# An earlier and denser routing of the third token block inside an attention loop

## The chip, the cores and the metric

The kernel runs on one core of a Trainium2 chip. The metric is the device time of one execution in microseconds (us). Before the change three runs took 1201.39, 1204.87 and 1204.54 us, a median of 1204.54 us.

The core's engines each have an in-order instruction queue of their own: PE (matrix products and transposes), DVE (vector operations), ACT (activations), POOL (general operations, and the DMAs that scatter or gather rows by an index), and SP, which issues the plain DMAs.

## The reference: what is computed

The reference adds four layers to `x`, each on normalised rows: an attention (2 sequences of 1024 tokens, 16 heads of 8), a mixture of 160 experts of which each token uses 8, a recurrent memory layer, and a second mixture of 8 experts. All is float32. The change touches the first two:

```python
scores = einsum('bhqd,bhkd->bhqk', qh, kh) * scale * decay      # decay by distance
x = x + einsum('bhqk,bhkd->bhqd', softmax(scores), vh) @ Wo
xn = layernorm(x)
probs = sigmoid(xn @ router_w.T + expert_bias)
top_w, top_idx = top_k(probs, 8)
h1 = silu(einsum('th,eih->eti', xn, w_gate))
x = x + routed(h1, top_w * 2.5, w_down, top_idx) + shared(xn)
```

## The kernel before

The 2048 tokens are 16 tiles of 128 rows, in four blocks of four tiles. A block's tokens can be routed as soon as their attention is done. Routing a block gives each of its tokens eight row numbers in a large buffer `xs` in HBM, ordered by expert: pages of 128 rows. Sending a token means copying its normalised row to those eight places. POOL does this: one indirect DMA sends 128 rows (one tile, one of its eight choices), so a block takes 32 such DMAs. In what follows, "a row" is one of these DMAs with the small memset (line 770) ahead of it. When all four blocks are sent, the experts work page by page.

**The attention** (`attention_bounded`) works in 16 units: a unit is 512 queries of one sequence and four heads. The loop over `s` runs through software-pipelined steps, nine to a unit; `u, k = divmod(s, 9)` is the unit whose exponentials are made, and `v` is the unit, 11 steps ahead, whose score maxima are made. The order of instructions is the one in which the code is written. One step does the following:

- `exps` and `largest`, in two halves: PE makes score tiles (L400); ACT exponentiates those of unit `u` (L383), DVE takes the maxima of unit `v` (L333). The maxima end with step 132.
- `product`, three steps later: PE multiplies by the values (L412). The partial results of even `k` are added by DVE (L422); those of odd `k` are copied by ACT from PSUM to the tile `part` (L425), of which there is one buffer, and added to `od` by POOL (L426). At `k` = 8 POOL adds the two sums (L428).
- at `k` = 5, `sums` of the unit before: PE collects the softmax denominators, DVE inverts them, and POOL spreads them over the partitions' columns (L438, `rb`). At `k` = 8, `divided` uses them on PE and DVE.
- once in each unit, `shift`: POOL adds the maxima to the queries (L305, L306).

The loop's end (after step 147) is `sums` and `divided` for the last unit, the rows that are still to be sent of those planned for the loop, and the last projection (L456, L459).

**Routing in the loop.** `route0(i, ...)` is a generator with 16 steps for block `i`. In order: 1, a reciprocal root on DVE; 2 and 3, two normalised tiles each on ACT (L659); 4, four transposes; 5 and 6, the router's products; 7, a clamp on POOL (L679); 8, two ACT passes for the sigmoid (L681, L682); 9 and 10, the top eight of two tiles each on DVE (L685, L686); 11 and 12, counts and positions by matrix products with four ACT passes in all (L706, L707); 13 and 14, page arithmetic on DVE; 15, an addition on POOL (L728); 16, the row numbers `idx` on DVE (L732). The blocks 0, 1 and 2 begin behind steps 47, 83 and 119, and the list `when` says at which distance from there a step of the generator is taken: one a step, 16 in a row. PSUM tiles of the generator come from the pool `ps_b`, four buffers that the exponentials' scores and the products use too.

**Sending in the loop.** `scattered(i, first, end)` is a generator with one row in each step (L770, L771). From step 64 on one row is sent behind each step: the formula gives the number of blocks that may send, and the first block with rows left sends one. Block 0 has the steps 64 to 95, block 1 the steps 100 to 131, block 2 the steps 136 to 143. Of block 2 the loop is given `SENT` rows: 12.

**Behind the attention** block 3 is routed by the same generator, with no attention beside it. Around it stand, in the order of the code: its first step, the loads of the expert weights (SP, L1441 and L1442, behind a DVE memset at L1439), the remaining rows of block 2 on POOL (`behind`, 32 - `SENT` of them), the shared expert of blocks 0 and 1 between the route's steps (L989 to L1001), then 32 rows of block 3 on POOL, which wait for L732. The load of the first page (SP, L1035) waits for the rows of all blocks.

Of the kernel before, what the change touches and what calls it, by code (L numbers as in the profile page):

```python
# [20 lines left out]
NB = T // 512  # L21
# [9 lines left out]

NE, INTER0 = 160, 64
ROUTED_SCALE = 2.5
SENT = 12
GAP = 6
SOME = 88
MORE = 128
# [139 lines left out]
def attention_bounded(tc, small, xnT, wq_sb, wkc, wvc, wo_sb, ident, x_sb, ln_stats,  # L177
# [11 lines left out]
    with tc.tile_pool(name="bw", bufs=1) as bw, tc.tile_pool(name="bk", bufs=1) as bk, \  # L189
# [58 lines left out]
        def second():  # L248

            own = x_sb[:, KT:NT, :]  # L250
            x1 = be.tile([P, KT, P], F32, tag="e", name="x1")
            nm, r, sq = [bq.tile([P, KT], F32, tag=f"s{n}", name=f"s{n}", bufs=1)
                         for n in range(3)]
            for i in range(KT):
                nc.scalar.activation(x1[:, i, :], own[:, i, :], AF.Identity,
                                     accum_out=nm[:, i : i + 1])
                if i == 3:
                    yield
            nc.vector.tensor_scalar(nm, nm, -1.0 / P, None, ALU.mult)
            yield  # L260
            for i in range(KT):
                nc.scalar.activation(x1[:, i, :], own[:, i, :], AF.Square,
                                     bias=nm[:, i : i + 1], accum_out=sq[:, i : i + 1])
            yield
            nc.scalar.activation(r, sq, AF.Sqrt, scale=1.0 / P, bias=eps_t)
            nc.vector.reciprocal(r, r)
            nc.vector.tensor_mul(nm, nm, r)
            yield
            for blk in range(2):
                pt = ps_b.tile([P, 512], F32, tag="b", name="pt")  # L270
                for j in range(4):
                    i = 4 * blk + j
                    nc.scalar.activation(x1[:, i, :], own[:, i, :], AF.Identity,
                                         scale=r[:, i : i + 1], bias=nm[:, i : i + 1])
                    nc.tensor.transpose(pt[:, j * P : (j + 1) * P], x1[:, i, :], ident)
                nc.scalar.copy(xnT[:, S + blk * 512 : S + (blk + 1) * 512], pt)
                yield
# [70 lines left out]
        def other(u):  # L348

            b, qb, g = units[u]  # L350
            ps = [pair("so") for _ in range(2)]
            for r in range(4):
                cols = slice(r * P, r * P + P)
                keys_of = slice((4 * qb + r) * P, (4 * qb + r) * P + P)
                for half in range(2):
                    for j in range(2):
                        rows = rows_of(half, j)
                        nc.tensor.matmul(ps[half][:, j, cols], ku[b, g][rows, keys_of],
                                         qu[u][rows, cols], start=True, stop=True)
            eo[u] = be.tile([P, 4, 512], F32, tag="eo", name="eo", bufs=1)  # L360
            for half in range(2):
                nc.scalar.activation(eo[u][:, 2 * half : 2 * half + 2, :], ps[half], AF.Exp)

        def exps(u, k, half):

            b, qb, g = units[u]
            kt = tile_of(u, k)
            if half == 1:
                es[u, k] = be.tile([P, 4, 512], F32, tag="e", name="e")
            e = es[u, k]  # L370
            ps = [ps_b.tile([P, 512], F32, tag="b", name="sb") for _ in range(2)]
            a = min(max(kt - 4 * qb, 0), 4) * P
            todo = []
            for k_, q_, lo, hi in ((ku, qu, 0, a), (kl, ql, a, 512)):
                for j in range(2):
                    if lo < hi:
                        rows = rows_of(half, j)
                        todo.append((ps[j][:, lo:hi], k_[b, g][rows, kt * P : (kt + 1) * P],
                                     q_[u][rows, lo:hi]))

            def after():
                for j in range(2):
                    nc.scalar.activation(e[:, 2 * half + j, :], ps[j], AF.Exp)  # L383

            return todo, after

        def whole(u, k):

            cols = slice((k - FIRST) * P, (k - FIRST + 1) * P)
            nc.vector.copy_predicated(es[u, k][:, :, cols],  # L390
                                      upp.bitcast(I32).unsqueeze(1).to_broadcast([P, 4, P]),
                                      eo[u][:, :, cols])

        def both(*work):

            work = [w for w in work if w]
            for n in range(0, max((len(w[0]) for w in work), default=0), 2):
                for w in work:
                    for out, lhs, rhs in w[0][n : n + 2]:
                        nc.tensor.matmul(out, lhs, rhs, start=True, stop=True)  # L400
            for w in work:
                w[1]()
# [27 lines left out]
        def sums(u):  # L430
            ps = ps_b.tile([P, 512], F32, tag="b", name="ps_r")[:, 0:16]
            for i in range(4):
                nc.tensor.matmul(ps[:, 4 * i : 4 * i + 4], os[u][:, i * P : (i + 1) * P],
                                 ident[:, HD::32], start=True, stop=True)
            ri = bo.tile([P, 16], F32, tag="ri", name="ri")
            nc.vector.reciprocal(ri, ps)
            ris[u] = bo.tile([P, 16, 32], F32, tag="rb", name="rb", bufs=1)
            nc.gpsimd.tensor_copy(ris[u], ri.unsqueeze(2).to_broadcast([P, 16, 32]))  # L438
# [13 lines left out]
        def projected(u, po):  # L452
# [8 lines left out]
            for i in range(4):  # L461
# [4 lines left out]
        LEAD, N, U = 11, 9, len(units)  # L466

        when = [1, 2, 3, 4, 5, 6, 7, 8, 9, 10, 11, 12, 13, 14, 15, 16]  # L470
        routes = [route0(i, lambda name: ps_b.tile([P, 512], F32, tag="b", name=name))
                  for i in range(NB - 1)]
        sent = [scattered(i, 0, 32 if i < NB - 2 else SENT) for i in range(NB - 1)]
        others = second()
        keys(0, 0)
        queries(0)
        end = N * U
        for s in range(-LEAD, end + 4):
            v, i = divmod(s + LEAD, N)
            u, k = divmod(s, N)  # L480
            second = 0 <= s < end and k > 0
            first = v < U and k > 0
            i8 = i - (i > 2)
            if i == 0 and 1 <= v <= U:
                nc.vector.tensor_reduce(pad[:, :, :, HD], mp.pop(v - 1), AX.X, ALU.max, negate=True)
            both(exps(u, k, 1) if second else None, largest(v, i8, 0) if first else None)
            if 0 <= s - 2 < end and 0 <= (s - 2) % N - FIRST < 4:
                whole(*divmod(s - 2, N))
            if 0 <= s - 3 < end and (s - 3) % N:
                product(*divmod(s - 3, N))  # L490
            if k == 0 and 0 <= s < end:
                other(u)
            if i == 2 and v + 1 < U:
                queries(v + 1)
            both(exps(u, k, 0) if second else None, largest(v, i8, 1) if first else None)
            if i == 0 and 1 <= v <= U:
                shift(v - 1)
            if k == 5 and 1 <= u < U:
                sums(u - 1)
            if k == 8 and 1 <= u < U:  # L500
                divided(u - 1)
            if v == 0 and i != 3:
                next(others, None)
            if v == 0 and i in (3, 8):
                values(i // 8)
            if i == 4 and 0 <= v < NG - 1:
                keys(0, v + 1)
            if k == 4 and 5 <= u < 5 + NG:
                keys(1, u - 5)
            if i == 4 and u - 2 >= 0 and units[u - 2][2] == NG - 1:  # L510
                projected(u - 2, pair("po")[:, 0, :])
            for blk in range(NB - 1):
                o = s - (N * (4 * blk + 5) + 2)
                for _ in range(when.count(o)):
                    next(routes[blk])
            blk = (s - (N * 5 + 2 + when[-1] + 1)) // (4 * N)
            if 0 <= blk < NB and s < end:
                for g in sent[: blk + 1]:
                    if next(g, sent) is not sent:
                        break  # L520
        sums(U - 1)
        divided(U - 1)
        for g in sent:
# [6 lines left out]
def model(ctx, tc, x, wq, wk, wv, wo, wdown, wupk, wupv, rw, ebias, wg, wd, wgs, wds,  # L530
# [249 lines left out]
    with tc.tile_pool(name="aw", bufs=1) as aw:  # L780
# [150 lines left out]
        with cond.Else():  # L931
# [11 lines left out]
            with tc.tile_pool(name="ps_r", bufs=4, space=PSUM) as ps_r:  # L943
                for i in range(NB - 1):
                    for _ in route0(i, lambda name: ps_r.tile([P, 512], F32, tag="r", name=name)):
                        pass
                    for _ in scattered(i, 0, 32 if i < NB - 2 else SENT):
                        pass
# [6 lines left out]
    with tc.tile_pool(name="fw", bufs=1) as fw, tc.tile_pool(name="fs", bufs=3) as fs, \  # L955
# [477 lines left out]
        with tc.manual_schedule():  # L1433
            last = route0(NB - 1, lambda name: ps_g.tile([P, 512], F32, tag="g", name=name))
            behind = scattered(NB - 2, SENT, 32)
            beside = [shared(i) for i in range(NB)]
# [186 lines left out]
```

## Time and profile before

One execution was profiled: its span, from the first to the last instruction, is 1197.7 us, and its own time was 1199.52 us, 5.0 us below the median of the runs.

| engine | busy us | share of the span |
|---|---|---|
| PE (products) | 990.6 | 83% |
| DVE | 766.8 | 64% |
| ACT | 627.8 | 52% |
| POOL | 538.1 | 45% |

The moments of this execution that matter here, in us from the span's start:

| moment | us |
|---|---|
| first exponential of step 131 (L383) | 566.2 |
| row numbers of block 2 (L732) | 586.5 |
| first exponential of step 143 | 607.5 |
| last spread of reciprocals (L438) begins | 617.53 |
| `x` complete (L459) begins | 624.01 |
| first weight load issued (L1441) | 636.99 |
| row numbers of block 3 (L732) | 661.35 |
| last row of block 3 begins (L771) | 702.87 |
| first page load issued (L1035) | 705.36 |

A profile line of the group view gives the line of the code, the engine, the operation, the names of what it writes and reads, the shapes and the count; then the busy time and the mean of one in ns; then the idle time of its engine just before it and who ended it. A line of the view in order of time gives start, duration, engine, line and operation, with the idle time ahead in brackets. "Clock" is the share of full speed that the chip granted to PE.

### The profile page before, as it was taken

What the parts mean: (1) busy time and instruction counts of PE and PEld (TensorE: products, weight loads), DVE (VectorE), ACT (ScalarE), POOL (GpSimd) and SP (SyncE); (2) the same over time, 40 slices, a digit from 0 to 9 for tenths busy, and PEclk for the clock granted to TensorE, in tenths of its full rate; (3) what the DMA queues carried; (4) which work ended last, traced back from release to release, by engine and by line L of the source; (5) the groups of instructions that cost most, each with busy time, mean ns of one, the idle gap of its engine ahead of it and who ended that gap; (6) DMA issues with size and microseconds to landing.
All of it is one profiled execution on the core that took longest, in us unless ns stands there. A gap on an engine that the chain in (4) does not pass through costs nothing. (4 is left out here: it accounts for less than half of the span.)

```text
span 1197.7 us, 20714 instructions
## 1 busy us (share of the span) xinstructions
PE 990.6 (83%) x7721; PEld 631.2 (53%) x7721; DVE 766.8 (64%) x1756; ACT 627.8 (52%) x1302; POOL 538.1 (45%) x657
## 2 busy tenths in 40 slices
PE   5899999998999999999972437888743479999998
PEld 2544444444444444554341226666632368888887
DVE  5788888677877798877534216555533457777643
ACT  3577777565766656666732014443322345666652
POOL 4345333344775735645556742232326565553000
PEclk9999999998999999999995558888775579999999
DMA  7999500000000000000007536776534212222110
GB/s 220 284 285 246 118 1 1 1 1 1 15 21 17 19 5 19 19 19 16 13 23 265 169 112 218 240 227 224 179 136 149 74 44 77 78 78 67 41 49 36
DMA packets 120334, 113.99 MB, mean 95 GB/s; under 512 B 50016, under 2 KB 102368, under 8 KB 118560
## 3 DMA queue, kind: packets, MB, share of 16 engines
q1 hardware_dynamic: 110496, 92.61, 25.3%
q0 software_dynamic: 9728, 19.94, 5.8%
q8 instruction: 66, 1.08, 0.4%
q14 instruction: 44, 0.36, 0.1%
HBM read 65.26 MB, written 57.74 MB: 103 GB/s over the span
## 5 line engine op out<-in xcount | busy, mean ns | idle before, releaser
L333 DVE TENSOR_REDUCE mp<-sa 128x2 f32<-128x1024 f32 x248 | 299.0, 1220 | 99.3 <-PE sa L400 94.1
L383 ACT ACTIVATE e<-sb 128x512 f32<-128x512 f32 x512 | 272.3, 601 | 116.5 <-PE sa L400 102.5
L400 PE MATMUL sa<-kl,ql 32*128 32x512 f32 (+3 forms) x752 | 172.3, 538 | 7.1 <-DVE mp L333 4.2
L400 PE MATMUL sb<-ql,kl 32*128 32x512 f32 (+3 forms) x768 | 171.1, 509 | 5.6 <-DVE o L422 3.7
L1407 POOL DMA_INDIRECT gt<-ys,idxu x128 | 122.6, 958 | 113.2 <-SPq L1473 25.4
L400 PE MATMUL sb<-qu,ku 32*128 32x512 f32 (+3 forms) x640 | 141.1, 507 | 6.0 <-DVE o L422 4.1
L412 PE MATMUL o_ps<-e,vv 128*32 128x512 f32 x1024 | 139.1, 616 | 3.8 <-DVE e L390 3.0
L400 PE MATMUL sa<-ku,qu 32*128 32x512 f32 (+3 forms) x612 | 124.5, 485 | 0.5 <-DVE mp L333 0.3
L400 PEld LDWEIGHTS sb<-ql,kl 32*128 32x128 f32 x768 | 74.3, 187 | 67.7 <-ACT e L383 32.7
L771 POOL DMA_INDIRECT xs<-xn,idxu x96 | 98.0, 1021 | 20.9 <-issue 17.7
L400 PEld LDWEIGHTS sb<-qu,ku 32*128 32x128 f32 x640 | 59.3, 185 | 88.9 <-ACT e L383 64.9
L1045 POOL DMA_INDIRECT wx<-wt,widx x48 | 46.0, 959 | 112.0 <-PE pt_x L1070 99.2
L426 POOL TENSOR_TENSOR od<-od,part 128x512 f32<-128x512 f32 x48 | 64.9, 1352 | 34.4 <-ACT part L425 34.0
L1373 ACT ACTIVATE hh_g<-gg_ps 128x512 f32<-128x512 f32 x64 | 37.9, 591 | 78.3 <-PE gg_ps L1360 62.9
L1364 PE MATMUL og_ps<-hw_g,w_sb 128*128 128x256 f32 x256 | 67.8, 388 | 3.9 <-DVE hw_g L1380 3.4
L1360 PE MATMUL u_ps<-xc,w_sb 128*128 128x256 f32 x256 | 69.2, 393 | 1.5 <-DVE xc L1355 1.3
L400 PEld LDWEIGHTS sa<-kl,ql 32*128 32x128 f32 x752 | 58.7, 186 | 21.1 <-DVE mp L333 9.3
L1360 PE MATMUL gg_ps<-x2T,w_sb 128*128 128x256 f32 x256 | 69.3, 395 | 0.0
L1380 DVE TENSOR_TENSOR hw_g<-hh_g,u_ps 128x512 f32<-128x512 f32 x64 | 43.7, 683 | 39.4 <-PE u_ps L1360 25.2
L1421 DVE SCALAR_TENSOR_TENSOR x_sb<-gt,w,x_sb 128x128 f32<-128x128 f32 x128 | 44.7, 350 | 29.8 <-DMA gt<-ys,idxu 25.4
L1070 PE MATMUL pt_x<-ident,xp 128*128 128x128 f32 x248 | 41.9, 322 | 26.5 <-DMA xp<-xs 24.4
L1127 DVE COPY y<-y_ps 128x512 f32<-128x512 f32 x31 | 21.4, 690 | 64.5 <-remote 29.9
(349 smaller groups left out, 1910.5 us busy)
## 6 DMA issues: line engine op xcount, KB each, us to landing
xs<-zeros SPq DMA_DIRECT2D x16, 1152.0 KB
xp<-xs SPq DMA_DIRECT2D x31, 512.0 KB
ys<-y SPq DMA_DIRECT2D x31, 512.0 KB
cb<-cD SPq DMA_DIRECT2D x8, 1024.0 KB
wt<-in_wg SPq DMA_DIRECT2D x4, 1280.0 KB
wt<-in_wd SPq DMA_DIRECT2D x8, 640.0 KB
wg_sb<-in_wg SPq DMA_DIRECT2D x4, 1280.0 KB
ys<-zeros SPq DMA_DIRECT2D x5, 512.0 KB
```

The lines of the kernel that those rows point to most:

```text
L333: nc.vector.tensor_reduce(mp[u][:, qt, 2 * half : 2 * half + 2, kb], pa, AX.X, ALU.max)
L383: nc.scalar.activation(e[:, 2 * half + j, :], ps[j], AF.Exp)
L400: nc.tensor.matmul(out, lhs, rhs, start=True, stop=True)
L412: nc.tensor.matmul(o_ps[32 * j : 32 * j + 32, :], vvs[b][:, kt, h : h + 2, :].rearrange("p a b -> p (a b)"), e[:, j, :], start=True, stop= ...
L426: nc.gpsimd.tensor_add(od[u], od[u], part)
L771: s = nc.gpsimd.indirect_dma_start(xs, bass.IndirectOffsetOnAxis(ap=idx[:, 4 * i + j, k : k + 1], axis=0), xn_[i][:, j, :], None).ins
L1045: dma = nc.gpsimd.indirect_dma_start(wx[:, q, :], None, wt, bass.IndirectOffsetOnAxis(ap=widx[:, c : c + 1], axis=0))
L1360: nc.tensor.matmul(ps[:, h, :], w13_sb[:, at : at + P], rhs, start=True, stop=True)
L1364: nc.tensor.matmul(o_ps, w2_sb[:, 2 * e + h, :], hw[e][:, h, :], start=(e == h == 0), stop=(e == NE1 - 1 and h == 1))
L1380: nc.vector.tensor_mul(hw[e], hh, u_ps)
L1407: dma = nc.gpsimd.indirect_dma_start(gt, None, ys, bass.IndirectOffsetOnAxis(ap=idx[:, t, k : k + 1], axis=0))
L1421: nc.vector.scalar_tensor_tensor(x_sb[:, t, :], rows[n], w8[:, t, k : k + 1], x_sb[:, t, :], ALU.mult, ALU.add)
```

## The change

`SENT` becomes 28, so 28 rows of block 2 are given to the loop and 4 remain behind it. A second list, `soon`, holds the distances for block 2: the same 16 steps of the generator in eleven steps of the loop (120 to 130), five of them taking two. From step 131 on two rows of block 2 are sent behind each step; the rule of before stays and sends one more from step 136 on. The other blocks, and the branch for other inputs but for the number `SENT`, stay as they are.

```diff
-SENT = 12
+SENT = 28
...
         when = [1, 2, 3, 4, 5, 6, 7, 8, 9, 10, 11, 12, 13, 14, 15, 16]
+        soon = [1, 2, 2, 3, 4, 4, 5, 6, 6, 7, 8, 8, 9, 10, 10, 11]
...
             for blk in range(NB - 1):
                 o = s - (N * (4 * blk + 5) + 2)
-                for _ in range(when.count(o)):
+                for _ in range((when if blk < NB - 2 else soon).count(o)):
                     next(routes[blk])
             blk = (s - (N * 5 + 2 + when[-1] + 1)) // (4 * N)
             if 0 <= blk < NB and s < end:
                 for g in sent[: blk + 1]:
                     if next(g, sent) is not sent:
                         break
+            if N * 13 + 2 + soon[-1] < s < end:
+                for _ in range(2):
+                    next(sent[NB - 2], None)
```

## The prediction

> **What bounds the kernel now.** The kernel is a row of stages, each waiting for the one before, so I read the stage that the change edits and the stage into which it reaches. The page's chain of waits starts at 886 us (the gathers after the pages) and can't be used here. So first the busy time by stretch of the last part of the attention: a unit without routing work, then from step 131's first exponential (566.2) to the copy L438 (end 618.14) that lets the last heads be divided, then up to the last block's row numbers.
>
> ```profile
> 479.20:510.30 31.10, 30.52 (x294) 15.36 (x290) 25.91 (x28) 21.98 (x41) 20.37 (x27) 1.00 0.06 21
> 566.20:618.20 52.00, 45.72 (x343) 19.96 (x340) 26.39 (x48) 32.25 (x60) 27.59 (x33) 1.00 0.04 13
> 618.20:662.40 44.20, 14.47 (x70) 11.57 (x70) 21.23 (x82) 8.33 (x15) 25.41 (x49) 0.58 0.62 213
> ```
>
> Columns: width, busy PE, PEld, DVE, ACT, POOL, granted clock, DMA share, GB/s. In a full unit PE is busy 30.5 of 31.1 us: PE bounds the attention. In its tail PE has 6 us idle, POOL 24. Then POOL's groups in that tail:
>
> ```profile
> L771 POOL DMA_INDIRECT xs<-xn,idxu x9 | 9.0, 1004 | 1.6 <-issue 1.6
> L426 POOL TENSOR_TENSOR od<-od,part 128x512 f32<-128x512 f32 x6 | 8.1, 1342 | 8.2 <-ACT part L425 8.1
> L428 POOL TENSOR_TENSOR o<-o,od 128x512 f32<-128x512 f32 x2 | 2.5, 1258 | 0.7 <-DVE o L422 0.6
> L438 POOL COPY rb<-ri 128x512 f32<-128x512 f32 x3 | 2.2, 725 | 14.9 <-DVE ri L436 14.9
> ```
>
> POOL sends rows and also adds up the attention's output (L426, L428) and spreads the reciprocals (L438); its idle time is waiting for those inputs. Last, POOL in order of time where the sent rows of block 2 end and those of block 3 begin, the DVE instruction that makes block 3's row numbers, and the first page load:
>
> ```profile
> 651.00 0.97 POOL L771 DMA_INDIRECT xs<-xn,idxu  x1 [0.22 <-issue]
> 651.98 0.09 POOL L770 MEMSET between<- 1x1 f32 x1
> 662.37 0.98 POOL L771 DMA_INDIRECT xs<-last,idxu  x1 [10.30 <-issue]
> ...
> 661.35 0.18 DVE L732 TENSOR_SCALAR idxu<-last 128x32 uint32<-128x32 f32 x1
> ...
> 705.36 0.70 SPq L1035 DMA_DIRECT2D xp<-xs  x1
> ```
>
> The 20 remaining rows of block 2 end at 652, and POOL then idles 10.3 us until DVE has the last block's numbers. From there 32 rows carry the path to the first page load. So the path is: attention's end, DVE's route of block 3, 32 rows, pages.
>
> **Part 1: sixteen rows leave the stretch behind the attention.** Back to back a row takes 1.27 us (memset starts 650.70 and 651.98), so POOL loses 16 x 1.27 = 20.3 us there. On the path this is worth nothing: POOL already waited 10.3 us for L732. What can gain is what those rows disturb. Their packets share the DMA engines with the expert weights loaded from 637 us on, and DVE L695 starts at 654.83 although its matmul's modelled end is 651 (a late release by PE that the trace doesn't explain). Bounds: 0 and -3.8 us, the whole late release. Three quarters of the rows lie under that load, yet similar late releases stand at 685 and 704 where the load is over, so I stay near nothing: **-1.0**. SP's queue is untouched: its loads start from a DVE memset (L1439) behind the first route step, and its first page load waits for the last rows.
>
> **Part 2: the route of block 2 in eleven steps.** No instruction is added; steps 12 to 16 move from attention steps 131-135 to 127-130. Their price in full attention steps is read from block 1, by the starts of each step's first exponential (L383): step 84 to 102 takes 376.5 to 454.4 = 77.9 us, the same positions without a route (21 to 39, 128.1 to 189.0) 60.9. A route costs 17.0 us, its steps 12 to 16 (95 to 102: 30.9 against 24.5) 6.4 of them. In the lighter tail, without the key maxima, the same five cost about 5.9: step 131 5.0 against 4.1, step 133 5.2 against 2.9, 134 and 135 7.2 against two of 2.85, step 137 3.4 against 2.2. Moving costs +0.5. Pairing adds in-order waits: DVE's maxima (step 9) now stand right behind ACT's two passes over pr (step 8: 0.74 + 0.83 us) in one step, with DVE's next score reduction queued behind them and PE behind that; steps 11 and 12 put 4 ACT passes (0.53 each) into one step and take three of the four PSUM buffers of the ring. Against it, fewer steps are disturbed. The trace has no paired step. Below: -3, since the two steps that cost 3 us each hold only 1.0 and 1.6 us of ACT work, the rest is interruption; above: +6, two 3 us hold-ups. By the nearest row, the 1.6 us of ACT work in front of DVE, partly saved elsewhere: **+1.0**. Sum of this part **+1.5**.
>
> **Part 3: 28 rows in the tail in place of 12.** Before, 8 fall into steps 136-143 and 4 behind the last copy. Now two go in each step from 131 and a third from 136 on (the old rule still fires): 2,2,2,2,2,3,3,3,3,3,3, all gone with step 141. Behind each row in POOL's in-order queue stand L426, L428, L438; and for them wait ACT (part has one buffer, so the next copy L425, with half a step's exponentials behind it, waits for L426) and PE (the sums wait for L428, the divisions for L438).
>
> Count from E, the start of step 131's exponentials. POOL begins at E+3.5 (L438 at 569.72). With block 1's last row, 29 rows x 1.27 = 36.8 us stand in the queue up to step 141, and between them two L438 (1.3), five L426/L428 (6.4) and the shift's two additions (2.5): 47.0, done at about E+50.6. Inputs come in time, the work always being ahead of POOL, so nothing idles. L426 of step 141 stands before that step's three rows: it ends about E+47. The copy L425 of step 143 waits for it, 10 us later than its place now (608.54, less the 5.9 us of route that leave the tail: E+36.5). Then in order: L426 (step 143) E+51.9, L425 0.6, L426 to E+53.9, L428 to E+55.2, sums, reciprocal and L438 as now (616.06 to 618.14: 2.1) to **E+57.3**. Now it is E+51.9 with the route in it, E+46.0 without. The rows cost **+11.3**. With rows at 1.31 us from memset to end (their mean at 300 to 450 us) and every final wait half again as long, about +14; if the adds found gaps, at least the overflow of rows alone: POOL's end E+50.6 plus 4.4 us of final adds, +9.
>
> Two rules of the Trainium skill speak against this part. "SBUF — State Buffer", section "SBUF: two separate sides", says that VectorE and GpSimd lock a shared port pair exclusively, so that a GpSimd-issued DMA can't write its descriptors while certain VectorE work runs; the example there is 0.62 us alone and 3.1 beside a copy. The rows here are 1.00 us mean in this tail, 1.03 to 1.05 mean earlier in the attention with DVE at 83%, 0.97 with DVE idle. By the rule's example twenty more rows could cost 62 us, by the row 25; I take the row. "TensorE: Matmul & The Clock Gate", section "Part 1: The HAM clock gate", says that an idle window of about 3.4 us halves the clock; the granted clock is 1.00 in this tail and 0.58 in the stretch behind it. The wait at E+42 to E+47 may now trip it: the last 16 products' matmuls at half speed would cost 1.5 us at most. By the row 0; I leave it in the range.
>
> **Sum.** -1.0 + 1.5 + 11.3 = +11.8 us. Against the profiled execution (span 1197.7, its own time 1199.5) that gives 1211.3; the median of the runs before is 5.0 above the profiled time, so against 1204.5 it is **1216.3**.
>
> **Rivals.**
> - *Faster: the rows were the disturbance.* The late release at 651 to 654.8 is caused by the rows' packets and goes (-3.8), and POOL's queue fits: it decides if the rows need under 0.9 us each (29 x 0.37 = 10.7 us less). 1204.5 - 3.8 + 0.5 = 1201, with a paired route at its best (-3) 1198. For it: POOL idles 24 us in the tail. Against: no row of the trace is under 1.2 us with its memset and gap, and most of that idle time lies ahead of the dependent adds. Chance 0.11. That POOL's 20.3 us were on the path (1184) the 10.3 us gap rules out.
> - *No change.* The queue drains by step 141 with half the delay, and Part 1 and the pairing give their best: +5 - 3 - 2, about 1204. Chance 0.08.
> - *Much slower: the paired steps hold up.* DVE, ACT and PE wait in a ring (+6) and the clock drops (+1.5): 1222.8, up to 1226 with Part 3 at its upper end. For it: in block 0 step 58 alone took 10.8 us. Against: data is one step old in most pairs. Chance 0.12.
>
> **Numbers.** The forecast's case has 0.69, from 1209 to 1221. Range: 1204.5 to 1224 leaves out the faster rival and the end of the slow one. Below 0.3% (3.6 us) a measurement can't tell a change from none: faster 0.11, same 0.10, slower 0.79.
>
> **What would show it.** POOL without gaps from about 577 to 624 with L426 and L438 waiting behind rows; L425 of steps 143 and 145 idle before, released by POOL L426; the last L438 at about 631; POOL idle some 30 us before block 3's first row, whose distance from the last L438 (44.2 us now) stays within 4 us; nothing moved from there on. I am wrong if POOL still idles in steps 136-141, or if the last L438 comes before 622.

## The result and the profile after

The changed kernel takes 1216.83 us (median of 8 runs), the kernel before 1203.33 us (8 runs): ratio 1.0116, 95% interval 1.0090 to 1.0143. The profiled execution has a span of 1211.9 us (its own time 1213.72). The forecast was 1216.3.

The same stretches as before, by window: a unit without routing, then from step 131's first exponential to the end of the last L438, then to the row numbers of block 3. Columns: window, width, busy PE, PEld, DVE, ACT, POOL, granted clock, DMA share, GB/s.

```profile
480.40:508.50 28.10, 27.52 (x266) 13.98 (x262) 23.89 (x27) 19.39 (x36) 17.78 (x24) 1.00 0.07 23
570.90:635.71 64.81, 54.15 (x336) 22.09 (x328) 19.98 (x37) 31.75 (x58) 45.52 (x71) 0.84 0.09 32
635.71:673.00 37.29, 14.58 (x70) 11.67 (x70) 19.22 (x74) 8.33 (x15) 4.36 (x9) 0.59 0.51 165
```

The tail is 64.8 us long (52.0 before). POOL is busy 45.5 us in it. PE runs hardly fewer matmuls in it (336 records, 343 before: part of block 2's route has moved ahead of it), but is busy 54.2 us for them (45.7 before) at a mean clock of 0.84 (1.00 before). The third stretch has become shorter, 37.3 us (44.2 before).

POOL's groups in the tail, where the number before the bar is the busy time and the last one the idle time ahead:

```profile
L775 POOL DMA_INDIRECT xs<-xn,idxu x29 | 29.1, 1003 | 6.0 <-issue 6.0
L426 POOL TENSOR_TENSOR od<-od,part 128x512 f32<-128x512 f32 x6 | 7.6, 1272 | 5.6 <-ACT part L425 5.5
L428 POOL TENSOR_TENSOR o<-o,od 128x512 f32<-128x512 f32 x2 | 2.5, 1275 | 0.1
L438 POOL COPY rb<-ri 128x512 f32<-128x512 f32 x3 | 1.9, 617 | 8.0 <-DVE ri L436 8.0
```

29 rows, one of them block 1's, at the same 1.00 us. In the order of time, where block 2's last rows go and block 3's begin, and the first page load (the code behind the loop has moved down by four lines):

```profile
648.21 0.99 POOL L775 DMA_INDIRECT xs<-xn,idxu  x1 [0.22 <-issue]
...
673.90 0.18 DVE L736 TENSOR_SCALAR idxu<-last 128x32 uint32<-128x32 f32 x1
674.92 0.98 POOL L775 DMA_INDIRECT xs<-last,idxu  x1 [25.64 <-issue]
...
717.84 0.34 SPq L1039 DMA_DIRECT2D xp<-xs  x1
```

POOL now idles 25.6 us before block 3's rows. The span put together from the starts of these instructions:

| stretch | before, us | after, us | difference |
|---|---|---|---|
| start to step 118 | 510.3 | 508.5 | -1.8 |
| step 118 to 131: the route of block 2 | 55.9 | 62.4 | +6.5 |
| step 131 to the end of the last L438: the tail | 51.9 | 64.8 | +12.9 |
| to `x` complete (L459) | 5.9 | 6.0 | +0.1 |
| to the row numbers of block 3 | 37.3 | 32.2 | -5.1 |
| to the last row, and to the first page load | 44.0 | 43.9 | -0.1 |
| to the end | 492.4 | 494.1 | +1.7 |

The total came out as forecast; its terms did not. The route cost four times what was put down for it, the rows that left the stretch behind the attention gave five times as much, and the tail's delay has only in part the cause that was given for it. The experiments take these terms one by one.

### The profile page after: what moved, and what is told of

It reads as the page before. It is cut to its first block, busy times and chain, and to the rows that moved or that the text cites. A ratio compares the mean times of both kernels' runs of the same rounds, so it can differ in the third digit from the quotient of the medians.

```text
span 1211.9 us, 20711 instructions
## 1 busy us (share of the span) xinstructions
PE 1000.2 (83%) x7721; PEld 635.3 (52%) x7721; DVE 763.7 (63%) x1756; ACT 629.2 (52%) x1302; POOL 537.4 (44%) x657
## 5 line engine op out<-in xcount | busy, mean ns | idle before, releaser
L383 ACT ACTIVATE e<-sb 128x512 f32<-128x512 f32 x512 | 272.6, 600 | 128.9 <-PE sa L400 106.0
L400 PE MATMUL sb<-ql,kl 32*128 32x512 f32 (+3 forms) x768 | 176.3, 517 | 7.5 <-DVE o L422 5.5
L400 PE MATMUL sa<-kl,ql 32*128 32x512 f32 (+3 forms) x752 | 172.7, 537 | 11.3 <-DVE mp L333 5.3
L1411 POOL DMA_INDIRECT gt<-ys,idxu x128 | 123.4, 964 | 111.2 <-issue 25.6
L426 POOL TENSOR_TENSOR od<-od,part 128x512 f32<-128x512 f32 x48 | 64.4, 1342 | 33.7 <-ACT part L425 33.2
```

Source lines behind the costliest of these rows:

```text
L426: nc.gpsimd.tensor_add(od[u], od[u], part)
L1411: dma = nc.gpsimd.indirect_dma_start(gt, None, ys, bass.IndirectOffsetOnAxis(ap=idx[:, t, k : k + 1], axis=0))
```

## The experiments

The kernels ran in three groups, each beside the kernel before: 1204.29 us (e1 to e4), 1149.25 (e5 to e8), 1202.95 (e9 to e12). The first and the third group ran on one chip, the second on another. The second chip is faster, mostly in the stages after the first page load, so ratios are read there, and the kernel before was not profiled on it. Stretches in us; "L695 late" is the time from its matmul's modelled end to its start.

| kernel | ratio to before, interval | 118 to 131 | tail | `x` to numbers | L695 late |
|---|---|---|---|---|---|
| before | | 55.9 | 51.9 | 37.3 | 6.2 |
| after | 1.0116 [1.0090, 1.0143] | 62.4 | 64.8 | 32.2 | 0.0 |
| e1 route alone | 1.0054 [1.0036, 1.0071] | 61.7 | 53.3 | 36.8 | 4.9 |
| e2 rows left out | 0.9937 [0.9917, 0.9958] | 56.3 | 54.5 | 32.2 | 0.0 |
| e3 rows at the end | 1.0104 [1.0067, 1.0142] | 62.5 | 53.1 | 45.8 | 0.0 |
| e4 additions on DVE | 1.0117 [1.0073, 1.0162] | 62.6 | 68.4 | 32.0 | 0.0 |
| e5 queue without rows | 1.0069 [1.0046, 1.0091] | 63.7 | 55.7 | 32.2 | 0.0 |
| e6 two a step | 1.0131 [1.0075, 1.0187] | 62.3 | 57.6 | 32.1 | 0.0 |
| e7 breaks behind | 1.0058 [1.0037, 1.0079] | 53.8 | 57.6 | 32.4 | 0.0 |
| e8 two a step, old route | 1.0004 [0.9979, 1.0030] | 53.8 | 56.4 | 32.5 | 0.0 |
| e9 before, beside | 1.0014 [0.9994, 1.0035] | 54.6 | 56.3 | 37.4 | 5.8 |
| e10 after, beside | 1.0110 [1.0073, 1.0147] | 63.7 | 64.3 | 31.9 | 0.0 |
| e11 longer queue without rows | 1.0098 [1.0067, 1.0128] | 62.6 | 58.1 | 31.9 | 0.0 |
| e12 one break | 0.9963 [0.9945, 0.9981] | 54.7 | 52.0 | 32.2 | 0.0 |

The same code does not give the same tail each time. Up to the tail's end the kernel before, e12, e2, e9 and e7 run the same code; their tails are 51.9, 52.0, 54.5, 56.3 and 57.6 us, at mean clocks of 1.00, 1.00, 0.94, 0.90 and 0.87. So the spread goes with the clock. Only the tail's last part, from the first exponential of step 142 to the end of the last L438, agrees in all five: 13.4 to 13.5 us. It is the safer measure of what waits for POOL.

**e1: the eleven steps alone.** Rows as before (12 in the loop).

```diff
-SENT = 28
+SENT = 12
...
-            if N * 13 + 2 + soon[-1] < s < end:
-                for _ in range(2):
-                    next(sent[NB - 2], None)
```

> Eleven steps alone, 12 rows as before. If the prediction's sum holds (0.5 for moving, 1.0 for pairing), +1.5 us against the kernel before: the stretch from step 118 to 131 longer by some 6.5 us, as in the changed kernel, and the tail from step 131 to the last L438 shorter by 5 to 6, at 46 us. If the paired steps are what costs, +6 us or more, with a tail that gives less than 3 back.

The route costs 6.5 us (0.0054 x 1204.29; 4.3 to 8.6); in the single traces steps 118 to 131 are 5.8 longer. By the starts of L383, step 125 to 127 takes 10.5 us (8.0 before) and step 130 8.2 (6.0). Next to nothing comes back in the tail: its first five steps, now without a route, take as long as before, 20.1 us against 20.4, though at a clock of 0.92; at a clock of 1.00 they take 19.8 and 20.0 in the two traces of the changed kernel. Windows of steps 131 to 135, first the kernel before, then e1:

```profile
566.20:586.60 20.40, 18.31 (x167) 8.32 (x165) 17.40 (x28) 13.05 (x24) 9.96 (x8) 1.00 0.02 5
```

```profile
570.00:590.10 20.10, 18.71 (x153) 8.61 (x154) 12.31 (x25) 12.10 (x22) 6.76 (x8) 0.92 0.03 8
```

DVE loses 5.1 us of work there, but PE was already busy 18.3 of 20.4 us: the route's DVE and ACT work lay under PE, and taking it away frees at most the 2.1 us in which PE had nothing to do.

**e2: sixteen rows left out.** The kernel before; rows 12 to 27 of block 2 are never sent.

```diff
-            behind = scattered(NB - 2, SENT, 32)
+            behind = scattered(NB - 2, SENT + 16, 32)
```

> The kernel before, with rows 12 to 27 of block 2 never sent (part of the routed tokens is missing from the experts' input), so that 4 rows remain behind the attention. By the prediction's Part 1 -1.0 us. If the rows cause the late release of DVE L695, -4 to -6 us, and L695 starts within 1 us of its matmul's modelled end. If that release is chance, it is late in this run as well, or early in other runs with 20 rows there.

The stretch from `x` to the numbers falls by 5.1 us, as in the changed kernel, and the time by 7.6 (5.1 to 10.0). L695 is on time. So on this chip the rows did disturb the route of block 3 although POOL had 10 us to spare.

**e3: the twenty rows after the last L438.** The changed kernel without its two-row rule; 28 rows are still given to the loop, and 20 of them fall behind its last division.

```diff
-            if N * 13 + 2 + soon[-1] < s < end:
-                for _ in range(2):
-                    next(sent[NB - 2], None)
```

> Eleven steps and 28 rows, but without the rule of two in a step: 8 in steps 136 to 143, 20 behind the last L438. If rows ahead of the additions are what costs, the 11 to 13 us of the tail are gone: between -4 and +2 us against before, tail at 46 to 48 us. If the number of rows costs wherever they stand, or the paired route does, it stays 8 us or more above before.

The tail is cured (53.1 us): it is the rows among the tail's work that lengthen it. But the time is that of the changed kernel, because the stretch behind grows to 45.8 us. The 20 rows, and the four that follow them, run from 627 to 658 with no gap over 0.7 us, and from some 13 us on DVE itself stumbles. DVE in order of time in the first route step of block 3:

```profile
652.16 0.16 DVE L654 TENSOR_TENSOR small_t<-small_t 128x4 f32<-128x4 f32 x1
653.49 0.16 DVE L655 TENSOR_TENSOR small_t<-small_t,small_t 128x4 f32<-128x4 f32 x1 [1.17 <-DVE small_t L654]
654.19 0.16 DVE L656 SCALAR_TENSOR_TENSOR small_t<-small_t,small_t 128x4 f32<-128x4 f32 x1 [0.54 <-DVE small_t L655]
655.59 0.16 DVE L654 TENSOR_TENSOR small_t<-small_t 128x4 f32<-128x4 f32 x1 [1.23 <-DVE small_t L656]
```

Instructions of 0.16 us stand up to 1.4 us apart, waiting for DVE's own results. The step takes 9.9 us (650.11 to 659.97), in the kernel before 2.4.

**e4: additions past the queue.** The changed kernel; for the last unit L426 and L428, and the last two L438, go to DVE.

```diff
-                nc.gpsimd.tensor_add(od[u], od[u], part)
+                (nc.gpsimd if u < U - 1 else nc.vector).tensor_add(od[u], od[u], part)
```

> The changed kernel, with the last unit's additions (L426, L428) and the last two spreads (L438) on DVE in place of POOL. Rows stay two or three in a step. If the cost is POOL's queue with the additions behind the rows, the tail falls from 64.8 to 45 to 48 us and the time to between -5 and +1 us against before. If the rows disturb by another way (descriptors, the DMA engines, PE's releases), the tail stays above 55 us.

Nothing waits for POOL any more at the end, and yet the tail is 68.4 us. A product that PE begins at 612.77, with a modelled end at 614.70, releases the ACT copy L425 only at 621.75. This made POOL's queue doubtful as the sole cause, and put the question what the rows do to PE's releases.

**e5 and e11: the queue without the rows.** The changed kernel; in place of each of the loop's rows 0 to 27 of block 2 POOL runs memsets, and these rows are never sent. From start to start a replaced row takes 1.16 us in e5 and, with one more small memset, 1.22 in e11 (a real one 1.26), so that e11's queue is still about 1 us short over the 28 rows.

```diff
             nc.gpsimd.memset(between, 0.0)
+            if not rows:
+                for _ in range(4):
+                    nc.gpsimd.memset(junk, 0.0)
+                yield
+                continue
```

> The changed kernel with the 28 rows of block 2 that its loop sends replaced by POOL memsets of about the same length (one small and four of 0.22 us, about 1 us in all, no DMA); so rows 0 to 27 of block 2 are never sent. POOL's queue stays as full as in the changed kernel, the row traffic of the tail is gone. If POOL's queue alone sets the tail (the prediction's Part 3), step 131 to the last L438 stays at 60 to 65 us and the time at 1213 to 1217. If the rows' traffic holds back PE's releases, the tail falls to about 53 to 55 us, no release by PE comes more than 1 us late in it, and the time is 1202 to 1206 (route +6.5 us, stretch behind the attention -6.4 us against the kernel before).

> The changed kernel with the 28 rows of its loop replaced by POOL memsets of now about 1.27 us from start to start (1.16 in e5), no DMA; rows 0 to 27 of block 2 are never sent. If POOL's queue alone makes the tail, step 131 to the last L438 is as in the changed kernel beside it, within 1.5 us. If the rows' traffic adds to it, it is 57 to 60 us, 5 us or more below the changed kernel beside it, and no release by PE is late.

e5 missed both of its cases: its tail of 55.7 us lies between them, and it is 8.0 us (5.3 to 10.5) slower than the kernel before. It ran on the second chip, where no trace has a late result (see below), so it can't tell what the traffic does; e11, on the first chip, can.

e11 is what the prediction described. First e11 in the order of time, then the changed kernel (E, the start of step 131's exponentials, is 572.8 and 570.9):

```profile
611.41 1.06 PE L412 MATMUL o_ps<-e,vv 128*32 128x512 f32 x8
612.57 0.69 DVE L422 TENSOR_TENSOR o<-o,o_ps 128x512 f32<-128x512 f32 x1 [3.53 <-PE o_ps L412]
...
618.64 1.26 POOL L426 TENSOR_TENSOR od<-od,part 128x512 f32<-128x512 f32 x1
619.93 0.58 ACT L425 COPY part<-o_ps 128x512 f32<-128x512 f32 x1 [4.29 <-POOL between L774]
...
630.26 0.61 POOL L438 COPY rb<-ri 128x512 f32<-128x512 f32 x1 [2.28 <-DVE ri L436]
```

```profile
610.47 1.06 PE L412 MATMUL o_ps<-e,vv 128*32 128x512 f32 x8 [1.70 <-issue]
...
618.21 1.27 POOL L426 TENSOR_TENSOR od<-od,part 128x512 f32<-128x512 f32 x1
618.39 0.69 DVE L422 TENSOR_TENSOR o<-o,o_ps 128x512 f32<-128x512 f32 x1 [12.28 <-remote]
...
619.86 2.29 ACT L383 ACTIVATE e<-sb 128x512 f32<-128x512 f32 x4 [5.15 <-remote]
...
623.22 0.59 ACT L425 COPY part<-o_ps 128x512 f32<-128x512 f32 x1 [1.07 <-PE o_ps L412]
...
630.21 1.27 POOL L426 TENSOR_TENSOR od<-od,part 128x512 f32<-128x512 f32 x1 [5.06 <-ACT part L425]
...
635.10 0.61 POOL L438 COPY rb<-ri 128x512 f32<-128x512 f32 x1 [2.28 <-DVE ri L436]
```

In e11 the addition L422 starts 0.1 us after its product, ACT's L425 waits for POOL's queue until E+47.1, and the last L438 ends at E+58.1. In the changed kernel POOL reaches the same L426 hardly later (E+47.3 against E+45.8), but L422 starts 6.9 us after its product's modelled end, ACT gets its scores 5 us late, and L425 then waits for PE, not for POOL. "Remote" means that no event of the trace explains the wait. In e10 the same L422 is 6.1 us late (product 613.17 to 614.23, L422 at 620.37). So of the tail, 53.3 us in e1, the queue adds 4.8 (58.1, at about the same clock: 0.92 and 0.91) and the rows' traffic another 6.2 to 6.7 (64.3 and 64.8). From step 142 on, where the same code agrees, the three are 13.6, 19.2 and 22.2 to 22.3. In the medians the traffic is worth 3.6 us (1213.46 against 1217.05), and the two intervals overlap: its share of the time is seen in the traces, not settled by the times.

In the same time PE's clock falls. Two windows of the changed kernel, 3.4 us just ahead and then the time at half the clock:

```profile
608.50:611.90 3.40, 1.70 (x13) 0.52 (x11) 0.00 (x0) 1.08 (x2) 2.73 (x7) 1.00 0.11 39
...
611.90:629.00 17.10, 13.40 (x44) 3.93 (x46) 3.70 (x5) 5.04 (x9) 11.32 (x18) 0.50 0.10 35
```

Ahead of the fall PE is busy only half of the time. Then it has half the clock for 17 us, and its last 24 matmuls of the products (626.05, 4.2 us) run in it. What the wait and what the clock costs can't be separated here. An estimate from the five tails of the same code (5.7 us for 0.13 of mean clock) makes about 3 us for the 0.07 between e11 and the changed kernel, so perhaps half of what is put down to the traffic is the clock.

**e6: two a step.** The changed kernel with 26 rows, and without the third in a step.

```diff
-SENT = 28
+SENT = 26
...
-                for g in sent[: blk + 1]:
+                for g in sent[: min(blk, 1) + 1]:
```

> The changed kernel with 26 rows in the loop, two behind each step from 131 to 143, without the third one from step 136 on; 6 rows remain behind. POOL's work (33.0 us of rows and 10.2 us of additions and copies) now fits into the tail with gaps. If the dense run of rows is what costs, the tail is 53 to 56 us and the time 1203 to 1207. If the number of rows in the tail costs (about 0.7 us for each of the rows beyond 8), it is 63 to 66 us and 1213 to 1217. A queue on POOL that never runs far ahead lies between, 56 to 59 us.

The tail is 57.6 us, 7 below the changed kernel's, though on another chip, and every L422 and L425 of its last ten steps starts within 0.4 us of its product's end. That does not show that the gaps cured anything: on this chip e7, with one row a step, has a tail of 57.6 us too, and no trace has a late result. What the rows cost through the queue is seen from step 142 on: 17.0 us, and 13.6 in e1. The ratio, expected near 1.00, is 1.0131 (4 runs). Against e8 on the same chip it is 8.5 us slower in steps 118 to 131 and 1.2 in the tail: the route again, which the expectation had left out.

**e7, e8 and e12: breaks between the rows.** The kernel before with breaks of POOL (memsets of one element) among the rows behind the attention: in e7 2.6 us more after every fourth of 20; in e8 the same among 16, four more being sent in the loop, two behind each step from 136; in e12 one break of 4 us after the twelfth of 20. The core of e12:

```diff
+            if paused and n > first and n - first == 12:
+                for _ in range(27):
+                    nc.gpsimd.memset(between, 0.0)
             nc.gpsimd.memset(between, 0.0)
...
-            behind = scattered(NB - 2, SENT, 32)
+            behind = scattered(NB - 2, SENT, 32, True)
```

> The kernel before, with its 20 rows behind the attention in groups of four and a break of 1.6 us or more (18 small memsets on POOL) between the groups. If an unbroken run of rows holds back PE's releases, L695 starts within 1 us of its matmul's modelled end (6.2 us late before), x complete to the row numbers of block 3 takes 32 to 34 us in place of 37.3, and the time is 1198 to 1201. If it is the number of rows or the weights' packets, L695 stays 4 to 7 us late, the last row ends later than before, and the time is 1203 to 1208.

> The kernel before, its route of block 2 untouched, with 16 rows in the loop (two behind each step from 136 on) and 16 behind in groups of four with breaks. If only unbroken runs cost: tail 51 to 54 us, L695 on time, 1197 to 1200, faster than both kernels. If POOL's queue costs in the tail, two rows (2.5 us) in front of each L426 make it 55 to 58 us and the time 1201 to 1205. If breaks do nothing, L695 is late by 3 us or more and the time 1202 to 1207.

> The kernel before with all its 20 rows behind the attention, and one break of about 4 us (27 small memsets on POOL) after the twelfth. If the unbroken run holds back PE's releases, L695 starts within 1 us of its matmul's modelled end where the kernel before beside it is 4 to 7 us late, and the time is 3 to 6 us below it (ratio 0.995 to 0.9975). If the number of rows or the weights' packets do it, L695 stays late and the ratio is 1.000 to 1.003. If the kernel before beside it has no late release, the break gains nothing: ratio 1.000 to 1.003.

In e7 L695 is on time, but the breaks are too long: the numbers of block 3 are there at 658.5, block 2's last row starts at 664.33, and block 3's rows wait 7 us (1 before). The time expected is missed. e8 ends its rows in time, and its interval holds both a gain and a loss. Its tail of 56.4 us lies within the spread of the unchanged code, but from step 142 on it takes 15.4 us where that code takes 13.5: two rows a step cost about 2 us there. That L695 is on time in both says little, for the reason that follows e12.

**e9 and e10: both kernels once more**, unchanged, beside e11 and e12.

> The kernel before, unchanged, for its stretches on the same chip as the next three kernels. If the late release of L695 belongs to the unbroken run of 20 rows, it starts 4 to 7 us after its matmul's modelled end here too, and x complete to the row numbers of block 3 takes 36 to 38 us. If it is a property of one chip (the rival: kernels with breaks gained nothing against the kernel before on a second chip), it starts within 1 us and the stretch takes 32 to 33 us. Step 118 to the last L438: 107 to 112 us either way.

> The changed kernel, unchanged, beside the kernel before on one chip. Step 131 to the last L438 about 65 us and PE's releases late while POOL sends rows without a gap, as seen before, if that holds on every chip: ratio 1.009 to 1.015. If the late releases of the tail belong to one chip, the tail is 57 to 60 us (POOL's queue alone).

They ran on the first chip again. So they settle that the late release is no property of one execution there, and leave open whether it belongs to that chip. DVE in order of time, e9, then e12:

```profile
648.85 0.60 DVE L689 TENSOR_SCALAR chosen<-mask 128x640 bf16<-128x640 f32 x1
655.95 0.33 DVE L695 TENSOR_TENSOR small_e<-pn_r,rows 128x160 f32<-128x160 f32 x1 [6.50 <-remote]
```

```profile
646.88 0.49 DVE L689 TENSOR_SCALAR chosen<-mask 128x640 bf16<-128x640 f32 x1
648.15 0.32 DVE L695 TENSOR_TENSOR small_e<-pn_r,rows 128x160 f32<-128x160 f32 x1 [0.78 <-PE pn_r L693]
```

L695 adds up four matmuls that start 0.6 us after L689. In e9, 20 rows follow each other from 627.8 to 653 and L695 waits 6.5 us; in e12 the same 20 rows have a gap from 641.2 to 645.7 and it waits 0.8. Number of rows, weight loads and route are the same; only the run is broken. The ratio of 0.9963 is a gain of 4.4 us (2.3 to 6.6): e12 is faster than both kernels.

**The chip.** Whether the late releases belong to one chip is seen in block 3's rows. In every kernel these 32 rows follow each other for some 40 us, with the work of the shared expert beside them. PE's last matmuls for an addition on DVE and that addition, first in the kernel before, then the same instructions in e8, on the second chip:

```profile
678.11 2.07 PE L999 MATMUL po_s<-wds_sb,hsh 64*128 64x128 f32 x8 [0.68 <-ACT hsh L996]
685.03 0.69 DVE L1001 TENSOR_TENSOR x_sb<-x_sb,po_s 128x512 f32<-128x512 f32 x1 [10.56 <-remote]
```

```profile
680.76 2.07 PE L1004 MATMUL po_s<-wds_sb,hsh 64*128 64x128 f32 x8 [0.68 <-ACT hsh L1001]
682.87 0.69 DVE L1006 TENSOR_TENSOR x_sb<-x_sb,po_s 128x512 f32<-128x512 f32 x1 [5.75 <-PE po_s L1004]
```

The rows began 15.7 us ahead of the first matmul in the one and 22.2 in the other, and take the same 41.5 us from the numbers to the last row. In the kernel before the addition starts 4.9 us after the modelled end, in e8 at once. So it is throughout: DVE and ACT wait longer than 1 us for "remote" 10 to 21 times in each trace of the eight experiments on the first chip and of the two kernels, whose times are those of that chip, and not once in the four traces of the second. The late releases belong to the first chip, or to a state of it; why, these traces don't say. So only e2, e3, e4, e11 and e12 tell something of the rows' traffic, and on the second chip the breaks had nothing to cure. That fits the times: e8 is as fast as the kernel before, and e7 is 6.7 us slower (4.3 to 9.1), where its breaks hold block 3's rows back by 6.

## Why the prediction came out right

**Part 1 (16 rows leave the stretch, -1.0): too small.** The trace gives -5.1, more than the bound of -3.8. The bound itself was misread: L695 waits for the matmuls of `pn_r` (L693), which end at 648.66, and 651 is the end of later ones, so the late release was 6.2 us long.

```profile
647.97 0.69 PE L693 MATMUL pn_r<-chosen,const 128*128 128x160 bf16 x4 [5.23 <-issue]
654.83 0.33 DVE L695 TENSOR_TENSOR small_e<-pn_r,rows 128x160 f32<-128x160 f32 x1 [6.91 <-remote]
```

That POOL's own time there is worth nothing held: it only idles longer (25.6 us). The argument against a larger gain failed: the late releases at 685 and 704 were taken as a sign that the rows are not the cause, because the weight load is over by then. But block 3's rows run there without a gap, and e12 shows that on this chip an unbroken run is what counts. That release lay on the path to L732, and most of what it held came back. No trace of the second chip has such a release, so there this term may be nothing; the two kernels were not compared on it.

**Part 2 (eleven steps, +1.5): wrong.** Moving the work was put at +0.5 because the light tail would give back 5.9. It gives next to nothing: the 5.9 compared single steps with other single steps, and the 18.3 us of PE in 20.4 set the length. At a clock of 1.00 and without the route, step 131 takes 5.2 us in the changed kernel (5.0 before), steps 134 and 135 take 7.3 (7.2) and step 137 takes 3.4 (3.4); only step 133 is shorter, 3.5 against 5.2, and step 132 is 0.8 longer. What the fuller steps cost was about right: 6.4 by block 1's row, 5.8 and 6.5 here, and 7.8 between the means of all traces (54.9 us for steps 118 to 131 in six with the old route, 62.7 in eight with the new). So the step that failed is the credit. Whether pairing costs something of its own (+1.0) can't be told from the rest; the hold-up of +6 in the last rival has the size of the whole.

**Part 3 (28 rows in the tail, +11.3): the size right, the cause half right.** After less e1 is 11.5 us. The count of POOL's queue was almost exact: without gaps from 576.1 to 623.4 (577 to 624 foretold), L426 of step 141 starting at E+47.3 (its end was foretold for about E+47), and in e11 the end at E+58.1 (57.3 foretold). But the tail without the rows was put at E+46.0, again by the credit of Part 2, and is 53.3 in e1 (at a clock of 0.92). The queue so costs 4.8 us, not 11.3. The other 6 to 7 are PE's late releases beside the unbroken run and the clock that falls with them, which nothing in the sum stood for: that the size fits is luck; and L425 of steps 143 and 145 waits for PE in the changed kernel, not for POOL L426.

**The two rules weighed.** The port between DVE and POOL: the row was right, 29 rows of 1003 ns with DVE at work. The Trainium skill's "TensorE: Matmul & The Clock Gate", section "Part 1: The HAM clock gate": the clock did fall, and the 0 us was wrong: it was at half for 17.1 us. But the window of 3.4 us ahead of it had PE busy for 1.7 us by the modelled ends, so it was not wholly idle as the rule has it, and in e9 the clock fell at 589.8, in code without the change, behind 3.4 us in which PE was busy throughout. That the wait made it fall is not shown.

**The rivals.** The first had the right mechanism in the wrong size: the rows were the disturbance, but in the tail they disturb as well. The second rival's sum took Part 1's best as -2 or so where its bound is -3.8, and would be about 1203 by its own terms. The drop of the clock in the last rival came true. The distance from the last L438 to block 3's first row went from 44.2 to 39.2 us, one more than the margin of 4, and from the first page load on nothing moved beyond 2 us.

The errors: -4 in Part 1, +5 in Part 2, and almost none in the size of Part 3, where two errors of 6 to 7 us stand against each other. They cancel by luck, and the total is right for reasons that were partly not its own.

## What to carry to other kernels

Before work that is moved out of a stage is credited, look which engine is busy there without it: where PE has 18 of 20 us, taking away DVE's work gains nothing. On one of the two chips, row DMAs that POOL issued one right behind another delayed the work of other engines though no one waited for the rows; where a trace shows such late results and the rows have slack, a break of a few microseconds is worth trying. An experiment on such an effect belongs on a chip that has been seen to show it: e5 to e8 ran on one that doesn't. And a total that fits says nothing of its terms: one run for each part found three errors in a sum that was right.

## What the runs showed of the hardware

On the first chip, while POOL issues rows one right behind another (in the tail with only its additions of 1.3 us in between), PE's results can reach the engines that wait for them 4 us and more after their modelled end: 6.9 and 6.1 us in the tail, 6.2 and 5.8 behind the attention, 7.0 in e4, and beside block 3's rows up to 17.2 (e11). Not every result is late: in the kernel before one that was ready 15 us into block 3's rows was used at once. In e3 DVE waits over 1 us for its own results. A break of 4 us removed the late L695 in e12, and memsets in place of the DMAs the late results of the tail in e11. On the second chip none of four traces has one, with the same rows at the same pace. Whether PE was done and its signal held back, or PE itself ran late, a trace with modelled ends can't say; why it happens, and why on one chip, stays open, and so does the shortest gap that suffices.

The granted clock can fall to half in the middle of the attention in one execution of a kernel and not in another: five tails of the same code took 51.9 to 57.6 us at mean clocks from 1.00 to 0.87.
